# Four conv-style layers on one core: image 0 of the self-attention layer with eight transposed runs, and its column sums on Pool

## The chip, the core and the metric

The kernel runs on one core of a Trainium2 chip. The metric is the device time of one execution in microseconds; the median of three runs stands for a kernel. Five engines work side by side: PE (TensorE, matrix products), DVE (VectorE), ACT (ScalarE), POOL (GpSimd) and SP (which here only issues DMAs). Each engine takes its instructions strictly in the order in which they stand in its own queue, and waits for other engines through semaphores.

## What is computed

Four images of 64 x 64 x 64 go through four layers: an attention layer with projections (layer 0), a convolution block (layer 1), an attention layer without projections (layer 2), and a non-local layer with batch norm (layer 3). The change is in layer 2, which for one image is

```
xf = x.reshape(B, C, N)                        # C = 64, N = 4096
scores = einsum('bci,bcj->bij', xf, xf)        # symmetric in i and j
attn = softmax(scores, axis=-1)
out = einsum('bcj,bij->bci', xf, attn) + x
```

All of it is in float32. The scores are symmetric, and since the kernel subtracts one constant before the exponential and divides by the row sums at the end, so are its exponentials.

## The kernel before, in words

**Blocks and steps.** Layer 2 of an image cuts its 4096 columns into eight groups h = 0 to 7 of 512. A step (h, g, u) makes a block of exponentials: four score products of 64x512 on PE (L1391, eight records in the trace), two exponentials of 128x512 on ACT (L1396), and, two or three steps later, four products of 64x512 with the image (L1453, eight records) that add to group h in PSUM. Steps u = 0 and 1 together are the block of group g against group h. Image 0 goes by the table `PART`, the other images by `FULL`.

**Transposed runs.** The block (g, h) is the block (h, g) turned. An entry that is a pair in the table, such as (1, 2), is a run: its four steps work as usual for group h, and besides DVE turns each block (L1409, into the tile `turned`), POOL's queue adds up its column sums, and then 64 small products of 32x64 by 32x256 on PE (L1479, 128 records) give what the pair's two groups get from group h. DVE adds these to the result A (L1492, or L1494 where A has nothing yet). So a run makes the steps of (g, h) for both groups of the pair needless. Image 0 has seven runs and 100 steps, the others fourteen runs and 72 steps.

**Column sums.** `column_sums` adds the turned blocks of a group into a tile `esum`. Usually POOL does it with a tensor add (L1432, from the second block on) and folds the halves (L1434). For image 0 a flag `moved` sends the groups after 0 by DMA instead: POOL only issues them (L1426, two interleaved chains, the third on waiting for the landing of the first), then a last DMA (L1430) and the fold L1434, each waiting for what went before. Nine steps after a group's last turned step (image 0) `spread_sums` turns the sum on DVE (L1442) and reduces it (L1443) into the small tile `cs`. At the first such group POOL clears `cs` (L1440).

**What sets the order.** The order of PE, ACT, DVE and POOL is the one in which the Python code issues the instructions: there is no other scheduler. `item(n)` issues a step: its score, its turning, its column sums, then convolution work that is due (two lanes, `conv` and `misc`, which go by a budget of microseconds per step), then due products, the 64 products of a run whose last step lies two or three back, and the spreading that is due. Beside layer 2 of image 0 runs layer 1 of image 3 (`conv`: norm at L1171 to L1192, pointwise products L1206, depthwise L1237 to L1252 on DVE, sum L1258 to L1277, second half L1289 to L1298), and near its end `features2(1)` (L1310 to L1314), which readies the tile `ko` for image 1. Layer 2 of image 1 follows.

**Buffers.** In this stage scores, runs and convolution take turns on three PSUM slots; a run takes two. Exponentials, sums `esum`, copies `own` of a finished group (L1465, added on DVE at L1468) and the weights `xr` of the runs share six buffers of one pool.

Of the kernel before, what the change touches and what calls it, by code (L numbers as in the profile page):

```python
# [691 lines left out]
def fast_path(ctx: ExitStack, tc: tile.TileContext, a: dict, out: bass.AP, bad):  # L692
# [43 lines left out]
    def piece():  # L736
        if turn_of["banks"]:
            return PS[:, bass.ts(new_bank(), 512)]
        return new_ps()[:, 0:512]
# [8 lines left out]
    def new_e(name="e"):  # L748
        return ep.tile([128, 2048], F32, tag="e", name=name)
# [4 lines left out]
    def new_big(name):  # L754
        return big.tile([128, 4096], F32, tag="big", name=name)
# [83 lines left out]
    for nm in names64 + names32:  # L839
        n = flat[nm].shape[0]  # L840
# [151 lines left out]
    def at(i, fn):  # L992
        due.setdefault(i, []).append(fn)
# [82 lines left out]
    between, late, steps, LAG = [], [], [], 6  # L1076
# [5 lines left out]
    def follow(lag=LAG):  # L1082
        if len(late) > lag:
            late.pop(0)()
# [218 lines left out]
    def features2(b):  # L1303
        x = X[:, b]
        im[b].ko = ko = new_big("ko")
        kv = ko[:, 0:N].rearrange("p (a e n) -> p a e n", e=2, n=128)
        for g in range(4):
            ps = piece()
            for i in range(4):
                nc.tensor.transpose(ps[:, bass.ts(i, 128)], x[:, bass.ts(4 * g + i, 128)], ident)  # L1310
            for e, copy in enumerate((nc.vector.tensor_copy, nc.scalar.copy)):
                own, other = slice(64 * e, 64 * e + 64), slice(64 - 64 * e, 128 - 64 * e)
                copy(kv[own, bass.ts(g, 4), e, :], ps[own, :].rearrange("p (a n) -> p a n", n=128))
                nc.sync.dma_start(out=kv[other, bass.ts(g, 4), e, :], in_=kv[own, bass.ts(g, 4), e, :])  # L1314
            yield 3.0
# [1 line left out]
    SIDES = [[(7, (h + 1) % 7), ((h + 2) % 7, (h + 3) % 7)] for h in range(7)]  # L1317
    FULL = [(7, [7])] + [(h, [h] + SIDES[h]) for h in range(6)] + [(6, SIDES[6] + [6])]
    PART = [
        (0, [0, 7, (1, 2), 5, (3, 4), 6]), (1, [1, 2, (5, 6), 3, 4, 7]), (2, [2, 1, 3, 4, 7]),  # L1320
        (3, [3, 1, 2, 4, 7]), (4, [4, 1, 2, 3, 7]), (7, [7, 0, 1, 2, 3, 4]),
        (6, [6, (2, 3), 0, (4, 7), 5]), (5, [5, (2, 3), (4, 7), 0, 6]),
    ]

    def layer2(b, when_free=None):
# [5 lines left out]
        steps, runs = [], []  # L1331
# [27 lines left out]
        def weights(h):  # L1359
            if "xr" not in st:  # L1360
                st["xr"] = (
                    new_e("xr") if b == 0 else new_pad("xr") if b == 1
                    else xn.tile([128, 2048], F32, tag="xn", name="xn")
                )
            for q in range(4):
                for k in range(4):
                    c = 1024 * (h % 2) + 256 * k
                    nc.sync.dma_start(
                        out=st["xr"][32 * q : 32 * q + 32, c : c + 256],
                        in_=x[32 * k : 32 * k + 32, 256 * h : 256 * h + 256],  # L1370
                    )
# [6 lines left out]
        def score(n):  # L1378
            h, g, u, _, _ = steps[n]
            if n == 0:  # L1380
                if b > 1:
                    take_slots(0, 1, 2)
                m.zs = sm.tile([128, 216], F32, tag="zs2", name="zs2")
            if n % 2 == 0:
                st["pair"] = new_e()
            e = st["e"][n] = st["pair"][:, bass.ts(n % 2, 1024)]
            ps = new_ps()
            for r, c in quads:
                rows_ = slice(64 * r, 64 * r + 64)
                k = 512 * g + 256 * u + 128 * r + 64 * c  # L1390
                mm(  # L1391
                    ps[64 * c : 64 * c + 64, bass.ts(r, 512)], m.ko[rows_, k : k + 64],
                    m.ko[rows_, bass.ts(h, 512)], start=True, stop=True,
                )
            for r in range(2):
                act(  # L1396
                    e[:, bass.ts(r, 512)], ps[:, bass.ts(r, 512)], AF.Exp, bias=SHIFT2,
                    accum_out=slot(g, 2 * u + r),
                )

        def turned(n):
            _, _, _, run, ti = steps[n]
            if run is None:
                return
            k = tile_of(run)
            if k not in st["T"]:
                st["T"][k] = new_big("turned")
            T = st["T"][k].rearrange("p (e s j) -> p s e j", e=16, s=8)
            nc.vector.transpose(  # L1409
                T[:, 2 * ti : 2 * ti + 2], st["e"][n].rearrange("p (s e i) -> p s e i", s=2, e=16)  # L1410
            )

        def column_sums(n):
            h, _, _, run, _ = steps[n]
            if run is None:
                return
            k, e = mine_t[h].index(n), st["e"][n]
            moved = b == 0 and h > 0
            if k == (0 if moved else 1):
                st["esum"][h] = new_e("esum")  # L1420
            if h not in st["esum"]:
                return
            esum = st["esum"][h][:, 0:1024]
            if moved:
                both = st["esum"][h]
                nc.gpsimd.dma_start(  # L1426
                    out=both[:, bass.ts(k % 2, 1024)], in_=e, **({} if k < 2 else {"accum_op": ALU.add})
                )
                if n == mine_t[h][-1]:
                    nc.gpsimd.dma_start(out=esum, in_=both[:, 1024:2048], accum_op=ALU.add)  # L1430
            else:
                nc.gpsimd.tensor_add(esum, st["e"][mine_t[h][0]] if k == 1 else esum, e)  # L1432
            if n == mine_t[h][-1]:
                nc.gpsimd.tensor_add(esum[:, 0:512], esum[:, 0:512], esum[:, 512:1024])  # L1434

        def spread_sums(h):
            if h == m.mirrored[0]:
                m.cs = sm.tile([128, 128], F32, tag="cs2", name="cs2", bufs=1)
                if b == 0:
                    nc.gpsimd.memset(m.cs, 0.0)  # L1440
            esum = st["esum"][h]
            nc.vector.transpose(esum[:, 512:1024], esum[:, 0:512])  # L1442
            nc.vector.tensor_reduce(  # L1443
                m.cs[:, bass.ts(h, 16)], esum[:, 512:1024].rearrange("p (e j) -> p e j", j=32), AX.X, ALU.add
            )
# [51 lines left out]
        def item(n):  # L1497
            if n in weights_at:
                weights(weights_at[n])
            score(n)  # L1500
            turned(n)
            column_sums(n)
            todo.append(n)
            if n == 2:
                m.A = new_big("A")
            if b == 0:
                for _ in range(2 if n < 3 else 1):
                    follow(0)
                if n == 2:
                    assert not late  # L1510
                conv.tick(1.5 if n in slow else 3.3)
                misc.tick(1.8)
            if n >= late_start:
                for _ in range(2):
                    if todo and todo[0] <= n - (3 if b == 0 and todo[0] in begin else 2):
                        products(todo.pop(0))
            for run, (_, _, last) in enumerate(runs):
                if n - (3 if b == 0 or run == 0 else 2) == last:
                    turned_products(run)
                    st["runs"] = st.get("runs", 0) + 1  # L1520
                    if run == len(runs) - 2 and when_free:
                        when_free()
            if n == len(steps) - 1:
                while todo:
                    products(todo.pop(0))
                assert st["runs"] == len(runs)
            if n in spread_at:
                spread_sums(spread_at[n])
# [284 lines left out]
    conv_from, misc_from, misc_to = {}, {}, {}  # L1813
# [9 lines left out]
    for b in range(B):  # L1823
        misc_to[len(items)] = True
        f = len(items)
        if b == 0:
            layer2(b)
            misc_from[f + 89] = [features2(b + 1)]
        else:
            layer2(b, lambda b=b: keys3(b - 1))  # L1830
            turns = close2(b - 1)
            for i in (10, 13, 22, 32, 42) if b == 1 else (8, 12, 22, 32, 42):
                at(f + i, lambda turns=turns: next(turns))
            misc_from[f + 46] = [open3(b - 1)]
            f = len(items)
            misc_to[f] = True
            layer3(b - 1)
            if b + 1 < B:
                turns = features2(b + 1)
                for i in (4, 7, 10, 13):  # L1840
                    between3[f + i] = 2, lambda turns=turns: next(turns)
    f = len(items)
# [220 lines left out]
```

## Time and profile before

| what | value |
|---|---|
| median of three runs | 2452.49 us (2452.43 to 2452.67) |
| the profiled execution's own time | 2456.51 us |
| its span in the trace | 2454.7 us |
| busy: PE, ACT, DVE, POOL | 98%, 67%, 60%, 22% |
| image 0's layer 2 in the trace, first score to image 1's first | 1017.0 to 1252.4 us |

The profile page gives busy times over the whole span; a matmul's busy time overlaps with that of its neighbours, so the distance between the starts of consecutive groups says more than the durations. In a timeline row stand the start in us, the length in us, engine, line, operation, tiles and shapes, the number of instructions merged, and in brackets the idle time before and what ended it.

### The profile page before, as it was taken

To read this page: it belongs to the slowest core of one execution; us is meant where nothing else is said; L and a number is where in the kernel's file an instruction comes from. 1 tells how busy PE (TensorE), PEld (TensorE's weight loads), DVE (VectorE), ACT (ScalarE), POOL (GpSimd) and SP (SyncE) were. 2 spreads that over 40 slices of the span, in tenths; PEclk is the share of its full clock that TensorE was granted. 3 is DMA by queue.
4 is the path that set the end of the run, shared out by engine and by line. 5 is a ranking of instruction groups with operands and counts; after the bars stand their busy time and mean duration, and the time that the engine had idled before them with its cause. 6 is when DMAs were issued, how large, how long until landed. Compare 5 with 4: busy or idle time off the path is not lost.

```text
span 2454.7 us, 63654 instructions
## 1 busy us (share of the span) xinstructions
PE 2417.0 (98%) x27509; PEld 916.3 (37%) x27509; DVE 1479.3 (60%) x1794; ACT 1644.3 (67%) x3140; POOL 540.9 (22%) x381
## 2 busy tenths in 40 slices
PE   9999999999999999999999999999999999999998
PEld 3343453336333633343334442144431344421113
DVE  2020278227832773378656668876668866678886
ACT  4656766676666676668654459954479744579996
POOL 2000000000000000120135561255631365622110
PEclk9999999999999999999999999999999999999999
DMA  3000000000000000120630027610075300286554
GB/s 80 1 18 1 19 1 18 18 19 1 18 18 16 4 19 18 35 63 2 136 72 20 19 67 134 139 27 23 16 150 119 78 20 20 71 168 142 120 118 117
DMA packets 66373, 131.68 MB, mean 54 GB/s; under 512 B 12860, under 2 KB 34085, under 8 KB 66085
## 3 DMA queue, kind: packets, MB, share of 16 engines
q0 software_dynamic: 23024, 81.83, 16.5%
q1 hardware_dynamic: 42309, 43.85, 7.9%
q8 instruction: 218, 3.57, 0.6%
q10 hardware_dynamic: 752, 1.85, 0.2%
q14 instruction: 70, 0.57, 0.1%
HBM read 4.80 MB, written 4.19 MB: 4 GB/s over the span
## 4 chain that ended last, share of the span: by engine, by line
PE 86%; DVE 8%; ACT 4%; issue 1%; SPq 0%; DMA 0%; DVEq 0%; ACTq 0%
PE PS L1096 18%; PE PS L1122 18%; PE PS L1391 10%; PE PS L1453 10%; PE PS L1646 8%; PE PS L1707 8%; PE PS L1479 7%; DVE tg L1698 3%; PE PS L1206 2%; ACT e L1657 2%; ACT e L1396 1%; DVE X L1568 1%; PE PS L1561 1%; PE PS L1064 1%; PE PS L1171 1%
## 5 line engine op out<-in xcount | busy, mean ns | idle before, releaser
L1101 ACT ACTIVATE e<-PS 128x1024 f32<-128x1024 f32 x512 | 524.2, 1024 | 339.4 <-PE PS L1096 306.3
L1396 ACT ACTIVATE e<-PS 128x512 f32<-128x512 f32 x632 | 371.6, 596 | 342.0 <-PE PS L1391 321.1
L1096 PE MATMUL PS<-X,q 64*64 64x512 f32 x4096 | 573.9, 591 | 2.3 <-DVE X L979 1.7
L1122 PE MATMUL PS<-e,vq 64*64 64x512 f32 x4096 | 575.3, 592 | 0.0
L1657 ACT ACTIVATE e<-PS 128x512 f32<-128x512 f32 (+2 forms) x588 | 500.2, 921 | 59.0 <-PE PS L1646 38.1
L1698 DVE TENSOR_TENSOR tg<-tg,e 128x2048 f32<-128x2048 f32 x172 | 393.8, 2290 | 42.8 <-ACT e L1657 30.9
L1391 PE MATMUL PS<-ko 64*64 64x512 f32 x2528 | 335.6, 596 | 2.6 <-DVE u L1291 1.5
L1453 PE MATMUL PS<-e,X 64*64 64x512 f32 x2528 | 329.9, 590 | 2.5 <-issue 1.4
L1432 POOL TENSOR_TENSOR esum<-esum,e 128x1024 f32<-128x1024 f32 x132 | 314.0, 2379 | 59.7 <-ACT e L1396 52.4
L1241 DVE SCALAR_TENSOR_TENSOR y<-pad,vec,y 128x1024 f32<-128x1024 f32 x240 | 308.8, 1287 | 18.2 <-ACT y L1237 10.9
L1432 POOL TENSOR_TENSOR esum<-e 128x1024 f32<-128x1024 f32 x22 | 52.2, 2373 | 1206.2 <-ACT e L1396 1187.3
L1409 DVE STREAM_TRANSPOSE turned<-e 128x1024 f32<-128x1024 f32 x196 | 240.6, 1238 | 106.0 <-ACT e L1396 105.8
L1646 PE MATMUL PS<-tg,ph 32*64 32x512 f32 x4096 | 295.1, 612 | 1.7 <-ACT e L1657 0.8
L1096 PEld LDWEIGHTS PS<-X,q 64*64 64x64 f32 x4096 | 183.0, 133 | 261.8 <-issue 181.6
L1122 PEld LDWEIGHTS PS<-e,vq 64*64 64x64 f32 x4096 | 183.1, 133 | 253.8 <-issue 158.1
L1707 PE MATMUL PS<-e,tg 128*32 128x512 f32 x2048 | 272.5, 604 | 0.0
L1109 DVE TENSOR_REDUCE sums<-zs 128x1 f32<-128x4 f32 x128 | 19.6, 153 | 276.4 <-ACT e L1101 276.2
L1679 POOL DMA_DIRECT2D xn<-e x116 | 101.0, 892 | 292.3 <-ACT e L1657 206.0
L1453 PEld LDWEIGHTS PS<-e,X 64*64 64x64 f32 x2528 | 98.0, 133 | 176.3 <-issue 156.7
L1391 PEld LDWEIGHTS PS<-ko 64*64 64x64 f32 x2528 | 90.5, 132 | 169.9 <-issue 145.7
L1646 PEld LDWEIGHTS PS<-tg,ph 32*64 32x64 f32 x4096 | 63.4, 129 | 222.9 <-ACT e L1657 190.5
L1396 ACT ACTIVATION_READ_ACCUMULATOR e<-PS 128x1 f32 x632 | 127.3, 201 | 0.0
(219 smaller groups left out, 1692.4 us busy)
## 6 DMA issues: line engine op xcount, KB each, us to landing
xn<-e POOLq DMA_DIRECT2D x132, 512.0 KB, 5.4
esum<-e POOLq DMA_DIRECT2D x20, 512.0 KB, 5.5
xn<-t SPq DMA_DIRECT2D x64, 128.0 KB
ph<-tg SPq DMA_DIRECT2D x64, 128.0 KB
xn<-X SPq DMA_DIRECT2D x224, 32.0 KB
xr<-X SPq DMA_DIRECT2D x176, 32.0 KB
ko<-ko SPq DMA_DIRECT2D x32, 128.0 KB
xr<-in_x_dram SPq DMA_DIRECT2D x13, 256.0 KB
```

What stands on the lines that cost most here:

```text
L1096: mm(ps[64 * c : 64 * c + 64, bass.ts(r, 512)], m.q[rows_, 128 * t + 64 * c : 128 * t + 64 * c + 64], x[rows_, bass.ts(g, 512)], start=Tru ...
L1101: act(es[g // 2][:, bass.ts(g % 2, 1024)], ps, AF.Exp, bias=SHIFT0, accum_out=zs[:, g : g + 1],)
L1122: ins = mm(PS[64 * s : 64 * s + 64, 2048 + 512 * j : 2560 + 512 * j], vq[rows_, :], es[j // 2][rows_, k : k + 512], start=t == 0 and i < 2 ...
L1241: stt(y1, win, wt, y1, ALU.mult, ALU.add)
L1391: mm(ps[64 * c : 64 * c + 64, bass.ts(r, 512)], m.ko[rows_, k : k + 64], m.ko[rows_, bass.ts(h, 512)], start=True, stop=True,)
L1396: act(e[:, bass.ts(r, 512)], ps[:, bass.ts(r, 512)], AF.Exp, bias=SHIFT2, accum_out=slot(g, 2 * u + r),)
L1432: nc.gpsimd.tensor_add(esum, st["e"][mine_t[h][0]] if k == 1 else esum, e)
L1453: mm(st["acc"][r][64 * c : 64 * c + 64, :], xw[rows_, 4 * g + 2 * u + c, :], st["e"][n][rows_, bass.ts(c, 512)], start=n == mine[h][0], st ...
L1646: mm(PS[64 * c : 64 * c + 64, bass.ts(banks[k], 512)], m.ph[32 * k : 32 * k + 32, 128 * mc + 64 * c : 128 * mc + 64 * c + 64], m.th[32 * k ...
L1657: act(e[:, 512 * lo : 512 * k], PS[:, 512 * banks[lo] : 512 * banks[lo] + 512 * (k - lo)], AF.Exp,)
L1698: nc.vector.tensor_add(esum, esum, e)
L1707: mm(st["y"][32 * k : 32 * k + 32, :], m.gx[:, i % 32, :], es[i][:, bass.ts(k, 512)], start=mc == 0, stop=i % 32 == 31,)
```

## The change

Image 0 gets an eighth run. The diagonal block of group 5 moves to the end of its row, behind its three runs; group 0 no longer takes group 5 by itself, nor group 6 group 5. Four steps go, 96 stay. The flag `moved` now holds for group 1 alone, so that groups 6 and 5, like group 0, are added by POOL. The last run's products are issued at the last step at the latest. `features2(1)` is due four items earlier, which is the same distance from the end.

```diff
     PART = [
-        (0, [0, 7, (1, 2), 5, (3, 4), 6]), (1, [1, 2, (5, 6), 3, 4, 7]), (2, [2, 1, 3, 4, 7]),
+        (0, [0, 7, (1, 2), 6, (3, 4)]), (1, [1, 2, (5, 6), 3, 4, 7]), (2, [2, 1, 3, 4, 7]),
         (3, [3, 1, 2, 4, 7]), (4, [4, 1, 2, 3, 7]), (7, [7, 0, 1, 2, 3, 4]),
-        (6, [6, (2, 3), 0, (4, 7), 5]), (5, [5, (2, 3), (4, 7), 0, 6]),
+        (6, [6, 0, (2, 3), (4, 7)]), (5, [(2, 3), (4, 7), (0, 6), 5]),
     ]
...
-            moved = b == 0 and h > 0
+            moved = b == 0 and h == 1
...
-                if n - (3 if b == 0 or run == 0 else 2) == last:
+                if n == min(last + (3 if b == 0 or run == 0 else 2), len(steps) - 1):
                     turned_products(run)
...
-            misc_from[f + 89] = [features2(b + 1)]
+            misc_from[f + 85] = [features2(b + 1)]
```

## The prediction

> **What bounds the kernel.** I read the page's busy shares first, then the chain that ended last, then PE's timeline through image 0's layer 2, then the other queues where PE had gaps.
>
> ```profile
> PE 2417.0 (98%) x27509; PEld 916.3 (37%) x27509; DVE 1479.3 (60%) x1794; ACT 1644.3 (67%) x3140; POOL 540.9 (22%) x381
> PE 86%; DVE 8%; ACT 4%; issue 1%; SPq 0%; DMA 0%; DVEq 0%; ACTq 0%
> ```
>
> PE sets the time nearly everywhere, so a saved matmul counts in full, and so does every gap on PE. What a step and a run cost is read from starts in PE's timeline:
>
> ```profile
> 1041.71 1.90 PE L1453 MATMUL PS<-e,X 64*64 64x512 f32 x16
> 1043.43 1.04 PE L1391 MATMUL PS<-ko 64*64 64x512 f32 x8
> 1044.29 1.04 PE L1453 MATMUL PS<-e,X 64*64 64x512 f32 x8
> 1045.25 3.71 PE L1479 MATMUL PS<-turned,xr 32*64 32x256 f32 x128
> 1048.89 1.09 PE L1391 MATMUL PS<-ko 64*64 64x512 f32 x8
> ```
>
> Eight records of a score or of a product occupy 0.86 us (1043.43 to 1044.29), so a step takes 1.72 us; the run takes 3.64 (1045.25 to 1048.89). PE's gaps in this stage are few until 1218, and then dense. The same view near the end of the stage:
>
> ```profile
> 1221.86 1.04 PE L1391 MATMUL PS<-ko 64*64 64x512 f32 x8
> 1223.85 0.66 PE L1310 MATMUL PS<-ident,X 128*128 128x128 f32 x4 [0.95 <-ACT ko L1313]
> ...
> 1237.45 1.02 PE L1453 MATMUL PS<-e,X 64*64 64x512 f32 x5
> 1239.85 0.64 PE L1453 MATMUL PS<-e,X 64*64 64x512 f32 x2 [1.37 <-issue]
> ...
> 1254.15 1.90 PE L1391 MATMUL PS<-ko 64*64 64x512 f32 x16
> 1257.51 1.09 PE L1391 MATMUL PS<-ko 64*64 64x512 f32 x8 [1.46 <-DVE u L1291]
> ```
>
> From starts minus 0.86 per eight records I count 1.1 (at 1218), 1.1, 0.8, 0.8, 1.9, 0.8 and 1.7 us: 8.2 us lost between 1218 and 1258, where features2, the norm of image 3, and the DMA sums of groups 6 and 5 meet.
>
> The last view is of the queues at group 1's sums, which stay on DMA:
>
> ```profile
> 1078.87 0.89 POOL L1426 DMA_DIRECT2D esum<-e  x1 [1.97 <-DMA esum<-e]
> 1079.44 0.54 POOL L1440 MEMSET cs<- 128x128 f32 x1
> 1080.40 0.87 POOL L1426 DMA_DIRECT2D esum<-e  x1 [0.42 <-issue]
> 1081.33 0.69 DVE L1443 TENSOR_REDUCE cs<-esum 128x16 f32<-128x512 f32 x1
> 1086.72 0.86 POOL L1430 DMA_DIRECT2D esum<-esum  x1 [5.45 <-issue]
> 1088.03 1.42 DVE L1494 COPY A<-PS 128x256 f32<-128x256 f32 x4 [2.38 <-PE PS L1479]
> 1091.62 1.47 POOL L1434 TENSOR_TENSOR esum<-esum 128x512 f32<-128x512 f32 x1 [4.04 <-DMA esum<-esum]
> ```
>
> The clearing of cs stands between the third and the fourth DMA, and group 0's reduction L1443 follows it at once. L1430 and L1434 each wait for a landing; the chain from the first DMA (1074.69) to the end of L1434 (1093.09) takes 18.4 us.
>
> **What the skill says.** The Trainium skill, "SBUF — State Buffer", section "Who interferes with whom", says that a DVE instruction with two SBUF inputs and a GpSimd instruction that reads SBUF shut each other out for a whole instruction. The trace agrees: with POOL's adds going, X+t took 2.37 us (1272.00) against a median of 0.69. I go by the trace: up to 1.7 us more for each L1277, L1468 or L1252 that meets an add. "TensorE: Matmul & The Clock Gate", section "What's actually happening", says that PE's clock halves after an idle window of about 3.4 us and returns after a busy one. The trace shows both: at the end of the span the granted clock went from 1.00 to 0.50 about 2.7 us after the last matmul (2444.2, drop at 2446.9), and at the start 64x512 matmuls took 1084 ns against 591 later, eight of them 1.92 us instead of 0.86, for the first 5 us or more of dense work. Inside the layers no gap of before is long enough, so this cost is not in the old time.
>
> **Part 1: four steps less, one run more.** -4 x 1.72 + 3.64 = **-3.2 us** of PE. The ACT work that goes (8 exponentials) and the DVE work that comes (4 turnings of 1.24 us, one L1492 group of 1.42) lie beside PE; in 1200 to 1250 DVE was busy 22.7 of 50 us.
>
> **Part 2: a new wait at the clearing of cs.** Group 0's row has two steps less, so group 1's turned steps are 18 to 21 instead of 20 to 23; the spreading of group 0 stays at step 22. So POOL's clearing, issued at step 22, now stands behind all of group 1's chain: four L1426, L1430, L1434. The built program's order on POOL confirms this. On DVE the queue is: turnings of 20 and 21, two L1241, L1442, L1443 (waits for the clearing), two L1244, then the four L1494 that empty the two PSUM slots of run (5, 6). On PE, after that run: score 25 in the third slot, one product, then score 26, which needs a slot that L1494 empties.
> By the rows of before: run (3, 4) starts half a step earlier, at 1062.2, and ends at 1065.8; score 18 starts at 1068.4, its exponentials end 2.27 us later, 1070.7: the first DMA. Plus 18.4 is 1089.1, the clearing 0.5: L1443 starts at about 1089.8, L1244 twice 1.33, two L1494: the slot is free at 1092.7. PE gets there at: score 18 at 1068.4, seven steps to 1080.4, the run to 1084.0, a score and a product to 1085.8. **+6.9 us** (5.5 to 8.5 for landings between 4.0 and 5.5 us). DVE loses 8.9 us of which PE loses 6.9; the depthwise work catches up in the 5.8 us that DVE waits for ACT at 1128.
> An idle PE of 6.9 us meets the clock drop. Slow for 3.4 to 6.8 us, at 0.86 against 1.92: 1.9 to 3.8 us lost. **+2.6** (0 if it doesn't drop).
>
> **Part 3: the end of the stage.** The DMA sums of groups 6 and 5 (16 L1426, 2 L1430) go; POOL does 18 adds of 2.38 and two folds of 1.27, 45.4 us, over 20 steps that with their four earlier runs and side work take some 57 us, so POOL keeps up; exponentials' buffers are reused at least four steps later, when their add is done. The runs now stand at steps 80, 84, 88, 92, 95, one between nearly every two transposes L1310, so that ACT and DVE have 3.64 us each time to finish ko. Following slot by slot with the durations above, I find no wait at ko, a wait of 0.6 to 3.0 us at the first L1310 (the L1492 before it stands behind L1277 and two L1468, which meet POOL's adds), and about 0.5 at the first L1206 of image 1's steps. 8.2 becomes about 2.5, and 0.7 for what such a count misses: **-5.0** (-8 to -2). SP's ko DMAs pass seven of the eight xn ones; ko lands ten us before image 1's scores need it.
>
> **Part 4: small terms.** L1252 at the end of the depthwise work can meet POOL's first add, and a fifth turning stands ahead of L1263: 0 to 2, I take +0.7. Image 3's tail lies four steps deeper in image 1's, where L1298, L1568 and a run come together: 0 to 1.5, +0.4.
>
> **Sum.** -3.2 + 6.9 + 2.6 - 5.0 + 1.1 = +2.4 us: span 2454.7 to 2457.1, and since the profiled execution (2456.51) lies 4.0 above the median, the median goes from 2452.5 to **2454.9**. Steps of 0.2%, 4.9 us, are about what a measurement of this kernel can tell from no change.
>
> **Rivals.**
> - *Forecast*, 2455, own range 2451 to 2459; chance 0.62 (of it 0.52 within 0.2%, 0.10 slower).
> - *Slower: POOL's adds lock DVE.* Eight L1277 and L1468 and two L1252 at up to 1.7 us more put L1263 and the evictions of runs late. From a delay of about 1.5 us per run on, PE waits at each eviction and the late gaps aren't reduced: -3.2 + 9.5 + 0 (instead of -5.0) + 2 = +8.3: 2461. For: the 2.37 us row. Against: DVE has more than half of that stretch free. Chance 0.20, slower.
> - *Late gaps vanish, early wait short.* Landings of 4 us, no clock drop, no late wait: -3.2 + 5.5 - 8.2 = -5.9: 2446.6. Chance 0.11 (0.07 faster, 0.04 same).
> - *No early wait*: L1443 is not held, or PE is not. -3.2 - 5.0 + 1.1 = -7.1: 2445.4. The row at 1081.33 right behind the clearing speaks against it. Chance 0.07 (0.05 faster, 0.02 same).
>
> Faster 0.12, same 0.58, slower 0.30; range 2447 to 2461.
>
> **What would show it.** A gap of 6 to 7 us before a score L1391 near 1086 to 1093, ended by DVE's L1494, with L1443 starting right behind L1440 near 1090, and a granted clock below 1 in the 5 us after; L1310 without waits for ko; L1277 and L1468 longer than 0.7. It is wrong if L1443 starts before 1085, if PE has several gaps behind runs, or if the late gaps stay.

## The result

The changed kernel is **slower by 12.2 us**: 2464.82 us (2463.78 to 2466.08, 6 runs) against 2452.58 (2451.61 to 2453.43, 6 runs), a ratio of 1.0050 (95%: 1.0039 to 1.0061). Forecast were +2.4 us, 2454.9, with a range of 2447 to 2461. The profiled execution took 2464.31 us, its span 2462.4.

The page of the changed kernel, busy times:

```profile
PE 2416.6 (98%) x27573; PEld 915.2 (37%) x27573; DVE 1493.7 (61%) x1803; ACT 1639.4 (67%) x3124; POOL 570.7 (23%) x381
```

PE is as busy as before, though it has 3.2 us less to do by Part 1, so the loss is idle time and slow matmuls. The timelines tell where. First the clearing of `cs`, on POOL, DVE and PE:

```profile
1086.89 1.26 POOL L1434 TENSOR_TENSOR esum<-esum 128x512 f32<-128x512 f32 x1 [4.15 <-DMA esum<-esum]
1088.09 0.20 POOL L1440 MEMSET cs<- 128x128 f32 x1
```
```profile
1088.32 0.69 DVE L1443 TENSOR_REDUCE cs<-esum 128x16 f32<-128x512 f32 x1 [8.58 <-POOL cs L1440]
...
1090.25 1.41 DVE L1494 COPY A<-PS 128x256 f32<-128x256 f32 x4
```
```profile
1083.86 1.04 PE L1453 MATMUL PS<-e,X 64*64 64x512 f32 x8
1091.05 1.99 PE L1391 MATMUL PS<-ko 64*64 64x512 f32 x8 [6.16 <-DVE A L1494]
1092.81 1.93 PE L1453 MATMUL PS<-e,X 64*64 64x512 f32 x8
1094.52 1.68 PE L1391 MATMUL PS<-ko 64*64 64x512 f32 x8
1096.03 1.03 PE L1453 MATMUL PS<-e,X 64*64 64x512 f32 x8
```

This is the forecast wait, link by link: fold, clearing, reduction, eviction, score. From the distances of starts less 0.86, PE loses 6.3 us before the score and 0.9 + 0.9 + 0.6 in the three groups after it: the granted clock is 0.50 from 1088.99 to 1095.82.

The other loss was not forecast. First two lines of DVE in the kernel before, where image 3's depthwise work ends:

```profile
1178.62 0.68 DVE L1468 TENSOR_TENSOR A<-own,A 128x512 f32<-128x512 f32 x1
...
1183.97 0.25 DVE L1265 TENSOR_SCALAR pw2s<-pw,ch 128x64 f32<-128x64 f32 x1
```

POOL, DVE and PE in the changed kernel, where group 6's sum now begins at that place:

```profile
1183.43 2.38 POOL L1432 TENSOR_TENSOR esum<-e 128x1024 f32<-128x1024 f32 x1 [95.15 <-ACT e L1396]
1187.87 9.67 POOL L1432 TENSOR_TENSOR esum<-esum,e 128x1024 f32<-128x1024 f32 x4 [2.05 <-ACT e L1396]
```
```profile
1183.52 2.85 DVE L1468 TENSOR_TENSOR A<-own,A 128x512 f32<-128x512 f32 x1
...
1187.62 0.16 DVE L1258 TENSOR_REDUCE ytot<-ysum 128x1 f32<-128x8 f32 x1
1187.70 5.74 DVE L1409 STREAM_TRANSPOSE turned<-e 128x1024 f32<-128x1024 f32 x5
1193.36 0.17 DVE L1263 TENSOR_SCALAR ch<-PS,vec 128x1 f32<-128x1 f32 x1
1193.57 1.58 DVE L1265 TENSOR_SCALAR pw2s<-pw,ch 128x64 f32<-128x64 f32 x1
```
```profile
1187.93 0.35 PE L1261 MATMUL PS<-ytot,sca 128*128 128x1 f32 x2 [0.75 <-DVE ytot L1258]
...
1195.21 1.97 PE L1270 MATMUL PS<-yg,pw2s 128*64 128x512 f32 x4 [3.34 <-DVE pw2s L1265]
1197.12 1.60 PE L1453 MATMUL PS<-e,X 64*64 64x512 f32 x8
```

L1468 meets POOL's first add and takes 2.85 us instead of its median of 0.69: it ends 0.56 after the add (1183.43 + 2.38 = 1185.81). L1258 is late by that, and PE waits 0.75 for it. Then L1263 stands behind five turnings (four in the kernel before), and L1265, a scaling of 128x64, takes 1.58 us instead of 0.25: the third of the four adds, at 9.67 / 4 = 2.42 each, ends at 1195.12, and L1265 at 1195.15. PE waits 3.34 us for it, and comes back slow: the four L1270 take 0.9 us more, from start to start, than in the kernel before, the product after them 0.5 more. A third place follows at the first L1310:

```profile
1218.71 1.11 PE L1310 MATMUL PS<-ident,X 128*128 128x128 f32 x4 [2.01 <-DVE A L1492]
1219.75 3.09 PE L1453 MATMUL PS<-e,X 64*64 64x512 f32 x16
```

DVE was late there because two L1468 took 3.45 us and two of the L1277 ahead of them 1.86 and 1.81. One of these L1277 met the last add of group 6. The other, and the slower L1468, met the first two adds of group 5 (lines for the same place stand below, at the early clearing). It costs 2.0 us of waiting, 0.5 on L1310 (1.11 for 0.66) and 1.2 on the two products. The waits for `ko` before L1310 are gone, as forecast. In all, the three waits are 0.75 + 3.34 + 2.01 = 6.1 us, and 0.9 + 0.5 + 0.5 + 1.2 = 3.1 us are slow clock.

### The profile page after: what moved, and what is told of

It is laid out like the page before. It is cut to its first block, busy times and chain, and to the rows that moved or that the text cites. A ratio compares the mean times of both kernels' runs of the same rounds, so it can differ in the third digit from the quotient of the medians.

```text
span 2462.4 us, 63761 instructions
## 1 busy us (share of the span) xinstructions
PE 2416.6 (98%) x27573; PEld 915.2 (37%) x27573; DVE 1493.7 (61%) x1803; ACT 1639.4 (67%) x3124; POOL 570.7 (23%) x381
## 5 line engine op out<-in xcount | busy, mean ns | idle before, releaser
L1432 POOL TENSOR_TENSOR esum<-esum,e 128x1024 f32<-128x1024 f32 x148 | 352.4, 2381 | 85.8 <-ACT e L1396 78.0
L1391 PE MATMUL PS<-ko 64*64 64x512 f32 x2496 | 332.5, 599 | 7.3 <-DVE A L1494 6.8
L1391 PEld LDWEIGHTS PS<-ko 64*64 64x64 f32 x2496 | 88.7, 133 | 174.5 <-issue 145.1
```

The lines of the kernel that those rows point to most:

```text
L1391: mm(ps[64 * c : 64 * c + 64, bass.ts(r, 512)], m.ko[rows_, k : k + 64], m.ko[rows_, bass.ts(h, 512)], start=True, stop=True,)
```

## The experiments

**Theory:** two costs, independent of each other: the late clearing of `cs`, and POOL's adds from group 6's first one on, which lock DVE (hold its instruction up until the add is done) where PE soon waits for it. **Rivals:** the new order (a fifth turning ahead of L1263, runs elsewhere) makes the late gaps; or the gaps of before that were to go were never in its median. In the kernels that clear `cs` early, lines from L1391 on lie 3 (the last lines 1) later: L1394 is L1391, L1469 is L1468.

**Before, once more.** No edit.

> The kernel before, unchanged, profiled once more. Its profiled execution took 4.0 us more than its median, and 4.4 us of the gaps that the prediction counted late in image 0's layer 2 (1.9, 0.8 and 1.7 us between 1237 and 1258) began with waits of PE and ACT that name nothing. If these gaps belonged to that one execution, this one shows about 2450.5 us of span and some 4 us of late gaps. If they belong to the kernel, the span is about 2454.7 again and the gaps are there.

Measured: 2452.46 us. Three waits for `ko` stand again (1.05, 1.12 and 0.83 us), and 0.82, 0.54 and 0.57 after them: 4.9 us instead of the 8.2 counted in the first profile. Of the two long waits of the first profile, the one that named no releaser (1.37) is absent, and the one for L1291 is 0.39 instead of 1.46.

So 3.3 of the 8.2 us belonged to that one execution, which was itself 4.0 us above the median. The three other kernels below with the old table agree: none has the wait of 1.37, and L1391 waits 0.39 to 0.40 us for L1291.

**The clearing early.**

```diff
+                if b == 0:
+                    m.cs = sm.tile([128, 128], F32, tag="cs2", name="cs2", bufs=1)
+                    nc.gpsimd.memset(m.cs, 0.0)
...
-            if h == m.mirrored[0]:
+            if h == m.mirrored[0] and b:
...
-                if b == 0:
-                    nc.gpsimd.memset(m.cs, 0.0)
```

The first part stands at the first step of layer 2, the rest in `spread_sums`.

> The changed kernel with the clearing of cs issued at the first step of image 0's layer 2, ahead of all sums; nothing else. If the wait of group 0's reduction for the clearing cost PE its gap of 6.3 us and the slow clock behind it 2.4 us, the time falls by 8 to 9 us, to about 2456. If the port between DVE and POOL is the main cost, it falls by no more than 3, since DVE would only be late elsewhere: about 2462 or more.

Measured: 2457.72 us (2457.06 to 2458.97), ratio to before 1.0020 (1.0011 to 1.0029): 7.1 us less than the change, where 8 to 9 were expected. The early gap and its slow clock are gone (6.3 + 2.4), but PE now loses 1.2 us near 1130, waiting for the copy `own`. In the change the gap had covered that wait; before has the like of it (0.83 us at 1099). The gaps from 1179 on stay: PE waits 3.33 us for L1265, which takes 1.58 again, and 1.99 us at the first L1310. DVE, then POOL, ahead of that wait:

```profile
1206.46 3.45 DVE L1469 TENSOR_TENSOR A<-own,A 128x512 f32<-128x512 f32 x2
```
```profile
1203.62 2.37 POOL L1435 TENSOR_TENSOR esum<-e 128x1024 f32<-128x1024 f32 x1 [1.66 <-ACT e L1399]
1206.70 2.66 POOL L1435 TENSOR_TENSOR esum<-esum,e 128x1024 f32<-128x1024 f32 x1 [0.71 <-ACT e L1399]
```

The first of these adds starts a sum anew (`esum<-e`): they are group 5's, so group 5 has a part in this loss.

**The sums of groups 6 and 5 on DMA.** In the changed kernel:

```diff
-            moved = b == 0 and h == 1
+            moved = b == 0 and h > 0
```

> The changed kernel with the sums of groups 6 and 5 by DMA again, as before; the clearing stays behind group 1's chain. If POOL's adds hold DVE up (L1468 2.85 us, L1265 1.58 us, L1277 up to 2.5 us in the changed kernel), the gaps of 0.8 and 3.3 us at L1261 and L1270 shrink to under 1.5 us together and the time falls by 3 to 6 us, to about 2460; the early gap of 6.3 us stays. If the new order of the runs makes the late gaps (a fifth turning ahead of L1263), the time stays within 2 us of 2464.8.

Measured: 2464.04 us (2462.18 to 2467.07), ratio 1.0049 (1.0032 to 1.0066). That is the number of the second reading, but not its reason: the waits that the adds made are gone. The wait for L1265 falls to 0.64 us, the one before L1310 is gone, and nothing is won, since PE has two new waits, of 1.92 and 1.52 us, near 1255 and 1260. The first, on PE and then on ACT:

```profile
1255.32 2.11 PE L1391 MATMUL PS<-ko 64*64 64x512 f32 x8 [1.92 <-ACT e L1396]
```
```profile
1254.58 0.60 ACT L1396 ACTIVATE e<-PS 128x512 f32<-128x512 f32 x1 [2.63 <-DMA esum<-e]
```

ACT has no buffer for its next exponentials until DMA sums have landed; at the second wait it stood 2.92 us. With the last group on DMA, the sum runs into image 1: the lock is traded for landings.

**POOL's adds in the old order.** The kernel before with only `moved` changed:

```diff
-            moved = b == 0 and h > 0
+            moved = b == 0 and h == 1
```

> The kernel before with only the flag changed: POOL adds the sums of groups 6 and 5; seven runs and the old order, clearing in its old place. If POOL's adds hold DVE up wherever they fall on the depthwise work's end and on the X+t additions, this is slower by 3 to 6 us: 2455.5 to 2458.5. If only the new order of the runs brings the late gaps, it is within 2 us of 2452.6.

Measured: 2459.19 us (2458.01 to 2459.88), ratio 1.0026 (1.0016 to 1.0037): +6.4 us, with the old table and four turnings ahead of L1263. Three instructions of DVE in a row meet adds:

```profile
1176.60 2.84 DVE L1252 SCALAR_TENSOR_TENSOR yg<-y,yg 128x512 f32<-128x512 f32 x1
...
1179.56 2.63 DVE L1468 TENSOR_TENSOR A<-own,A 128x512 f32<-128x512 f32 x1
...
1186.86 1.67 DVE L1265 TENSOR_SCALAR pw2s<-pw,ch 128x64 f32<-128x64 f32 x1
```

That is 2.15 + 1.95 + 1.42 = 5.5 us later than in before; PE waits 3.90 us. The new order isn't needed for it, and the cost is a little above the 3 to 6 us expected.

**Both costs out, sums on DMA.** The two edits above together, in the changed kernel.

> The changed kernel with cs cleared at the first step of image 0 and the sums of groups 6 and 5 put back on DMA, so with both suspected costs taken out and only the eight runs left. If the early wait and POOL's adds are the two causes and nothing else is: the early gap of 6.8 us before a score goes with its slow clock (-9 us against the version with DMA sums alone, 2464.0), so 2455, and what stays above before is the waits of ACT for the landings of the DMA sums near 1250 (2.1 and 3.3 us on PE). If the two costs overlap or the clock recovers anyway: 2457 to 2461. If the new order by itself is good and the DMA landings move off when the early gap goes: 2450 to 2452.

Measured: 2457.88 us (2456.82 to 2458.84), ratio 1.0020 (1.0012 to 1.0028). It is 6.2 us below the version with DMA sums alone, but stays 5.1 above before: ACT's waits for landings (3.3, 2.1 and 2.6 us) hold PE at three places (0.3, 1.4 and 2.2 us), the last with slow clock after it. Two of the three readings were too low. The time lies in the third, 2457 to 2461, but its reason (the two costs overlap) doesn't hold: the clearing is worth 6.2 us here and 7.0 to 7.1 in the other pairs, and it is the landings that keep the time up.

**Clearing early, group 6 on DMA, group 5 by POOL.**

```diff
-            moved = b == 0 and h == 1
+            moved = b == 0 and h in (1, 6)
```

with the early clearing.

> The changed kernel with cs cleared at the first step, group 6's sum on DMA and only group 5's (and 0's) by POOL. If POOL's adds of group 6 lock DVE where the depthwise work of image 0 ends, the gaps there (1.1, 3.5, 0.8, 2.2, 1.3 us) go to under 2 us in all, and group 5's adds, which stand beside little DVE work that PE waits for, keep the DMA landings off the end of the stage: 2449.5 to 2451, faster than both kernels by some 2 to 3 and 14 us. If the gaps come from the order of the runs and a fifth turning instead of the adds: they stay, and 2456 to 2458. If group 6's DMA landings hold the exponentials' buffers as with both groups on DMA: 2453 to 2455.

Measured: **2449.61 us** (2448.50 to 2450.39), ratio 0.9985 (0.9979 to 0.9992): faster than both kernels, as the first reading had it. L1469 is 0.69 at most, L1265 is 0.25. What is left in that place is the fifth turning:

```profile
1185.32 1.08 PE L1270 MATMUL PS<-yg,pw2s 128*64 128x512 f32 x4 [0.84 <-DVE pw2s L1265]
```

**The late clearing alone,** in the kernel before:

```diff
-        spread_at = {mine_t[h][-1] + (5 if b else 9): h for h in m.mirrored}
+        spread_at = {mine_t[h][-1] + (5 if b else 11 if h == 0 else 9): h for h in m.mirrored}
```

> The kernel before with the spreading of group 0, and with it the clearing of cs, two steps later, at step 24, behind all of group 1's chain on POOL; nothing else is changed. If the wait for the clearing is by itself what cost 6.3 us and then 2.4 us of slow clock in the changed kernel: a gap of 6 to 7 us before a score near 1090, a granted clock below 1 in the 5 us after, and 2460 to 2462 (+8 to +9 us). If the changed row (the run of group 5 and 6 earlier by two steps) is needed for PE to wait: under 3 us of gap, no drop of the clock, 2453 to 2455.

Measured: 2460.63 us (2460.18 to 2462.28), ratio 1.0033 (1.0021 to 1.0045): +7.8 us, with a wait of 5.66 us of PE for L1494 and 1.4 of slow clock after it. The new row is not needed for it.

**POOL without reading.** The changed kernel with the early clearing, and for groups 6 and 5

```diff
-                nc.gpsimd.tensor_add(esum, st["e"][mine_t[h][0]] if k == 1 else esum, e)
+                if b == 0 and h in (6, 5):
+                    nc.gpsimd.memset(esum, 1.0)
+                else:
+                    nc.gpsimd.tensor_add(esum, st["e"][mine_t[h][0]] if k == 1 else esum, e)
```

> The changed kernel with cs cleared at the first step and with POOL's tensor adds of groups 6 and 5 replaced by memsets of the same tile, as many; the column sums of these two groups are left out, and the exponentials' buffers are no longer held by POOL. If POOL's reading of SBUF is what locks DVE: L1265 is back at 0.25 us, L1468 and L1277 at 0.7, the gap of 3.5 us before L1270 is gone, and 2449 to 2451. If POOL's writing is enough, or the order of runs is the cause: the gaps of 3.5 and 2.2 us stay and the time is 2456 to 2458.

This kernel leaves out the column sums of the two groups. Measured: 2451.25 us (2450.25 to 2453.74), ratio 0.9994 (0.9985 to 1.0002): 6.5 less than with the adds. The expectation was too simple, though. The memsets wait for no exponentials and run in two bursts, with each group's fold, which does read. POOL, then DVE:

```profile
1177.32 1.60 POOL L1440 TENSOR_TENSOR esum<-esum 128x512 f32<-128x512 f32 x1
1185.54 11.04 POOL L1436 MEMSET esum<- 128x1024 f32 x11 [6.62 <-DVE turned L1412]
```
```profile
1177.72 1.76 DVE L1472 TENSOR_TENSOR A<-own,A 128x512 f32<-128x512 f32 x1
...
1186.69 0.86 DVE L1265 TENSOR_SCALAR pw2s<-pw,ch 128x64 f32<-128x64 f32 x1
...
1190.44 0.69 DVE L1277 TENSOR_TENSOR X<-X,t 128x512 f32<-128x512 f32 x1 [1.22 <-ACT t L1275]
```

L1472 (L1468 of the others), with two inputs in SBUF, is held by the fold, which reads (1.76 for 0.68, ending 0.56 after the fold). L1277, of the same kind, is not held by memsets, which only write: 0.69, against 2.48 beside the adds of the version with early clearing. But L1265, with one tensor input, is held by a memset: at 11.04 / 11 = 1.00 us each, the second of them ends at about 1187.55, and L1265 at 1187.55. So in this execution reading held the addition, and for the scaling, writing was enough; each rests on one instruction. The remaining wait of PE fits: 1.0 of gap as with group 6 on DMA, 1.1 from L1472 and 0.6 from L1265 make 2.7, and 2.69 is measured (from starts). The profiled execution took 2453.17 us, 1.9 above the median, so these waits and their slow clock needn't be in every execution.

**Only group 5 to POOL, in the kernel before** (it has seven runs, not nine): `moved` as in the fastest version, nothing else.

> The kernel before, with its nine runs and its order, and only group 5's sum moved from DMA to POOL. It tells what of the 3.2 us by which the changed kernel with the early clearing and group 6 on DMA (2449.6) beats before comes from the eight runs and the new order, and what from POOL's adds for group 5. If from the four steps less and from runs that cover the waits for ko: the three waits for ko of 1.1, 1.1 and 0.8 us stay here and the time is that of before, 2452 to 2453. If from taking DMA landings out of the end of the stage: 2449.5 to 2450.5.

Measured: 2452.74 us (2451.89 to 2454.55), ratio 1.0000 (0.9992 to 1.0008). The three waits for `ko` stay. POOL's adds for group 5 alone cost nothing and bring nothing here, where they start behind group 6's chain on POOL, at 1216.57; the gain of the fastest version comes with the new table.

**Only group 6 back on DMA, in the changed kernel:** the same edit, the clearing late.

> The changed kernel with one edit: group 6's sum is on DMA again; the clearing of cs stays late. If the two costs stand for themselves: the early gap of 6.3 us and its slow clock stay, the gaps at the end of the depthwise work shrink to one of about 1.0 us before L1270, and the time is 2449.6 + 7.1 = 2456.7 (2456 to 2458). If group 6's landings meet the work that the early gap has delayed: 2459 to 2462.

Measured: 2456.57 us (2455.26 to 2457.80), ratio 1.0014 (1.0008 to 1.0021), as expected. It completes a table, in the new order, with group 5 on POOL throughout:

| | group 6 on DMA | group 6 by POOL |
|---|---|---|
| clearing early | 2449.61 | 2457.72 (+8.1) |
| clearing late | 2456.57 (+7.0) | 2464.82 (+15.2) |

The two costs add up within 0.2 us. The second column also moves group 5's adds forward: its first starts at 1203.6 in the version with early clearing, and at 1209.0, behind group 6's chain, in the fastest. So the 8.1 us are the price of group 6's switch, not of its seven adds alone; no run separates them. With before at 2452.6, the change is -3.0 + 7.0 + 8.1 = +12.1, and 12.2 was measured.

## Why the prediction was wrong

- **Part 1** (four steps less, one run more, -3.2). Right as far as it can be told: with both costs taken out the new table is 3.0 us (against the runs of before made beside it, 3.2) faster than before. That the total comes so close to this one term is in part chance, see the last point.
- **Part 2** (+6.9 and +2.6). Right in mechanism and place: L1443 starts at 1088.3 (forecast 1089.8), and the gap is 6.3 and the slow clock 2.4 us. Net it costs 7.0 to 7.1, not 9.5: later, the gap covers the 1.2 us lost at `own`; the rest of the difference wasn't traced.
- **Part 3** ("8.2 becomes about 2.5 [...] **-5.0**"). This step failed, in two ways. First, its 8.2 us came from one execution. The second profile of the same kernel has 4.9. The prediction took off these 3.3 us as gaps that would go, and then another 4.0 to come from that execution to the median: much the same time, subtracted twice.
  Second, it followed the lock only from L1277 and L1468 to the L1492 before L1310. That wait came as foreseen ("0.6 to 3.0", measured 2.0), but without the 1.7 us of slow clock behind it. And the same lock hits twenty-odd us earlier, where a single chain runs through DVE: L1468, L1252, L1258, L1263, L1265, and PE's L1270 behind it.
- **Part 4** ("0 to 2, I take +0.7" for L1252 at the first add and a fifth turning ahead of L1263). The fifth turning alone costs 1.0 us (the gap that is left with group 6 on DMA). The lock makes L1468 longer by 2.2 us and L1265 by 1.3, on one chain, and PE then idles long enough to be slowed, a term the prediction gave to the early wait only. By the lines of the change this place loses 0.75 + 2.5 of waiting beyond that 1.0 and 1.4 of slow clock, the first L1310 2.0 + 1.7: 8.4 us together, where the switch costs 8.1.
- **Part 4, image 3's tail**, +0.4. In the fastest version PE loses some 3.9 us in short gaps between 1242 and 1290 (0.6, 0.3, 1.2, 0.6, 0.6, 0.6), where before's second profile has 1.1. Together with 1.0 at L1270 this about takes back the 3.0 for `ko` and the 0.8 at a run. So without either cost, Part 3 and Part 4 come to about zero. This is read from the traces; no run separates it.

The sum: Parts 3 and 4 were -5.0 + 1.1 = -3.9, and were 12.2 + 3.2 - 7.1 = +8.3. Of these 12.2 us of error (by chance the size of the whole change), 3.3 are the gaps counted twice, 8.1 come with group 6's sum on POOL, and 0.8 is left for the rest. Part 2 was 2.4 too high, so the sum was off by 9.8 only.

Of the rivals, **"POOL's adds lock DVE"** named the cause and even L1263, but let PE wait "from a delay of about 1.5 us per run on", at the evictions of runs, and came to 2461. What decided was one chain of DVE, L1468 to L1265, between two matmuls of PE. "DVE has more than half of that stretch free" was no argument against it: the share of busy time doesn't tell whether the next instruction PE waits for stands behind a locked one. The other two rivals fail at the first place, where both the wait and the slow clock came.

**The list of what meets an add** came from one half of a page of the Trainium skill, "SBUF — State Buffer", section "Who interferes with whom": two SBUF inputs against a POOL instruction that reads. The same section says that `tensor_scalar` can enter a mode in which it uses both ports, and that DVE in such a mode contends with GpSimd. L1265 is a `tensor_scalar`; that it was in this mode no trace shows. The times fit both halves: 2.48 against 0.69 us for L1277 beside an add and beside memsets, and 0.25, 0.86 and 1.58 us for L1265 beside neither, beside a memset and beside an add. A list made from the whole section would have had L1265 on it.

## What to carry to other kernels

When work moves to POOL, list every DVE instruction that runs beside it, scalings included, and follow those that PE waits for soon after; price each at up to the rest of the POOL instruction that it meets (up to 2.2 us here), several in a row, and not by DVE's free time. Then price PE's slow clock behind every wait of about 2 us. Before counting gaps as something to be won, see whether they are in a second execution, and never subtract both a gap and the distance of its execution from the median. A clearing can be put far ahead of a queue that waits for landings: here this alone was worth 7 us.

## What the runs showed of the hardware

PE's clock dropped after much shorter idle times than expected. The Trainium skill's page "TensorE: Matmul & The Clock Gate", section "What's actually happening", speaks of a window of about 3.4 us, and the prediction looked for gaps near that. In the version with early clearing, an idle time of 2.0 us was enough. Windows of that trace (from and to, length, busy us of PE, PEld, DVE, ACT and POOL, granted clock, DMA share, GB/s):

```profile
1209.70:1211.75 2.05, 0.07 (x4) 0.00 (x0) 2.05 (x5) 1.93 (x5) 0.52 (x1) 1.00 0.00 0
1213.00:1214.60 1.60, 1.60 (x12) 0.39 (x12) 1.08 (x2) 0.48 (x1) 0.59 (x1) 0.50 0.00 0
```

The clock falls to 0.50 at 1211.88, just after PE has started again, and stays there for 3.41 us. The granted clock in the twelve traces shows a pattern after the first 20 us. Before the end of the work, each low stretch lasts 3.41 us or twice that. The falls of one trace stand whole multiples of 3.413 us apart: in the change at 1088.99, 1194.80 and 1218.70, which are 31.0 and 7.0 times 3.413. So each trace can be cut into stretches of 3.413 us that end where a fall can come. The clock fell at the end of every full-clock stretch in which PE had been idle for 1.92 us or more (1.92 with DMA sums, 1.99 above, 2.01 in the change at 1218.70, and longer ones), and of none with 1.64 us or less (1.64 with the late clearing alone, 1.46 before, 1.42 with DMA sums and early clearing). Between 1.64 and 1.92 there is no case. What counts is the idle time within one stretch, so a gap of 2 us that lies across the end of one might do nothing; no trace has such a gap. Behind two of the three late waits of the change the slow clock cost 1.4 and 1.7 us, 3.1 of the 9.2 us lost at these places.
